# Attention gated by a dequantized FFN: Wo's row factors taken on ScalarE, an earlier schedule for gates and the last queries, and half a projection finished later

## The chip, the core and the metric

The kernel runs on one core of a Trainium2 chip. The metric is the device time of one execution in microseconds. Before the change three runs gave 1065.36, 1066.66 and 1067.37 us, a median of 1066.66 us.

## What is computed

The reference, cut to what matters (S = 1024 tokens, DM = 512, 32 query heads, 8 key and value heads, head size 128, FF = 1792):

```python
xn = _layernorm(x)
q = rmsnorm(split_heads(xn @ Wq.T), q_norm_w)          # 32 heads
k = rmsnorm(split_heads(xn @ Wk.T), k_norm_w)          # 8 heads
v = split_heads(xn @ Wv.T)
bias = where(rel > 0, -1e30, slopes * rel)             # causal, a slope per head
attn = softmax(q @ k.T / sqrt(128) + bias)
s = merge_heads(attn @ v) @ Wo.T
gate = silu(xn @ dequant(gate_w)); up = xn @ dequant(up_w)
g = silu((gate * up) @ dequant(down_w))
return x + s * g
```

## The kernel before

Everything runs in four engines' hand-written order: what a source line issues first stands first on its engine, and nothing is reordered. Floats go through the matrix engine as pairs of f16 (a high and a low part), so each product is three matmuls (`mm3`, L112). ScalarE usually makes the high part and VectorE the low one.

**The FFN** (0 to about 217 us) comes first. Its result, the gate, is stored to DRAM (`gd`), 256 KB for 128 tokens.

**Twelve projections** follow (about 217 to 490 us): for each pair of key heads one of kind `kv` and two of kind `q`, k = 0 to 11. Each has eight tiles of 128 tokens (`tile`, L570): twelve matmuls of 512 columns into one PSUM bank, `o` for odd tiles and `m` for even ones, two buffers each; ScalarE copies the bank to SBUF (`f`) and sums its squares (`jk`), and for `kv` VectorE makes the values' low half (`v`, L595). Every four tiles `queue_half` (L767) queues a finish: `inverse` and `newton` (the roots: a few small operations on VectorE and twelve on GpSimd), then per tile `normalize` (GpSimd, L636), two steps later `halves` (VectorE, a cast L648 and a subtraction L649), then `transposed` (a DMA transpose on SyncE's queue, L657) and `store` (L662). `finish_step` (L477) runs what is due at each step of a clock; it counts one for each tile and one for each attention step.

While projection k runs, `prepare` (L671) makes the weights of k+1 ready, at tile t: `norms` at t = 1 (a small matmul into a spare bank, then VectorE), `scale` at 2, `split_head` i at t = 2 + i (ScalarE `wh` L561, VectorE `wl` L562), `split_values` at 4 and 5, `factors` at 6; at t = 6 also the squares of k+2 (ScalarE). The spare bank is one of tag `m` (`spare`, L486). A projection's first tile needs all of `wh` and `wl`.

**Attention** has 256 steps, 32 to each group g (one key head and four query heads). A group is cut into blocks of eight steps by query block qb of 256 tokens, in the order 2, 3, 0, 1 (group 0: 3, 2, 1, 0; group 7: 2, 3, 1, 0); a step is one head and one tile of 128 queries against (2 qb + 1 or 2 qb + 2) x 128 keys, so qb3 steps are the longest. `step(n)` (L1018) issues: scores of n on the matrix engine into a bank pair `s`; for step n-1 the bias and row minimum (VectorE, `pf` L878) and the exponential (ScalarE, L879); for n-3 the scaled high half `p` (ScalarE, L898); for n-4 the low half (VectorE, L907) and the DMA transpose into `pT` (SyncE's queue, L915 or L910); for the unit of n-9 the product with V (`av`); the output projection `op` and its sum `y` (VectorE, L980). Steps 0 to 7 run among the tiles of projections 10 and 11. In qb0 blocks GpSimd clears `p` first (L894).

**Wo's rows**: 32 tiles of 128x512, four a group. `load_wo` (L832) issues the DMA on SyncE's queue at the end of a step, `scale_wo` (L836) multiplies by a factor for each partition two steps later on GpSimd, `split_wo` (L839) two steps after that (ScalarE `woh` L843, GpSimd `wol` L844). In groups 1 to 7 these stand in the qb3 block and the one after it.

**Projection 11** (the queries of group 7) is not stored: `LAST_ROOTS` and `LAST_PAIRS` (L56) give the attention steps of its roots and of its eight tiles' `halves` (`normalize` two steps before), and `LAST_QUERIES` those of the transposes from SBUF straight into `qT` (L817). Its `f` tiles stay in SBUF until then; the tag has three buffers.

**Gates**: `GATE_LOADS` are the steps at which a query block's gate and x (two DMAs of 512 KB, L962 and L963) are loaded into an `f` buffer, `GATE_SUMS` those at which GpSimd forms y times gate plus x (L969, L970; two tiles, four operations).

Of the kernel before, what the change touches and what calls it, by code (L numbers as in the profile page):

```python
# [10 lines left out]
F32 = mybir.dt.float32  # L11
F32R = mybir.dt.float32r
F16 = mybir.dt.float16
BF16 = mybir.dt.bfloat16
I32 = mybir.dt.int32
AF = mybir.ActivationFunctionType
ALU = mybir.AluOpType
# [4 lines left out]
P = 128  # L22
S = 1024
DM = 512
# [3 lines left out]
HD = 128  # L28
FF = 1792
NI = FF // P  # L30
# [5 lines left out]
NQT = QB // P  # L36
# [16 lines left out]
VALUES_STEP = 24  # L53


LAST_ROOTS = {1: 24, 0: 36}  # L56
LAST_PAIRS = {4: 46, 5: 78, 6: 110, 7: 142, 2: 174, 3: 221, 0: 224, 1: 229}
LAST_QUERIES = {4: 217, 5: 219, 6: 225, 7: 227, 2: 233, 3: 235, 0: 241, 1: 243}

WO_SPLIT = 6  # L60
WO_SCALE = 8
WO_LOAD = 10

GATE_LOADS = [211, 219, 235, 251]
GATE_SUMS = [227, 235, 251, 259]
PF_BUFS = 5
P16_BUFS = 5
OH_BUFS = 8
# [8 lines left out]
def attention_gated_by_ffn_kernel(ctx, tc, x, gu_w, gu_z, gu_s, dn_w, dn_z, dn_s, wq, wkv, wo, qnw, knw, out):  # L77
    nc = tc.nc
    ve, se, ge, te, sp = nc.vector, nc.scalar, nc.gpsimd, nc.tensor, nc.sync
# [5 lines left out]
    def ps2(name):  # L85
        return psum[0].tile([P, 2, 512], F32, tag="s", name=name)

    def ps1(tag, name):
        return psum[0].tile([P, 512], F32, tag=tag, name=name)
# [22 lines left out]
    def mm3(ps, lhs, rhs, first, last):  # L112
        (lh, ll), (rh, rl) = lhs, rhs
        te.matmul(ps, lhsT=lh, rhs=rh, start=first, stop=False)  # L114
        te.matmul(ps, lhsT=lh, rhs=rl, start=False, stop=False)  # L115
        te.matmul(ps, lhsT=ll, rhs=rh, start=False, stop=last)  # L116
# [12 lines left out]
    rvs = const.tile([P, HKV], F32, name="rvs")  # L129
# [30 lines left out]
    def pair(name):  # L160
        return fpsum.tile([P, 2, 512], F32, tag="pair", name=name)
# [267 lines left out]
    def dn_dequant(it, engine=ge):  # L429
        wi, wf, zi, si = dn_raw[it]  # L430
        ve.tensor_tensor(wf, wi, zi, ALU.subtract)
        engine.tensor_tensor(wf, wf, si, ALU.mult)
# [9 lines left out]
    def dn_split_h(it, tb):  # L442
        hh = gp.tile([P, 512], F32R, tag="hh", name=f"hh{it}_{tb}", bufs=3)
        hl = gp.tile([P, 512], F32R, tag="hl", name=f"hl{it}_{tb}", bufs=3)
        split_r(h[:, it, tb * 512 : tb * 512 + 512], hh, hl)
        dn_h_hl[it, tb] = (hh, hl)
# [36 lines left out]
    def defer(steps, f):  # L483
        finishing.setdefault(clock[0] + steps, []).append(f)

    def spare(k, name):  # L486
        return ps1("m", name) if k else pair(name)[:, 0, :]

    class Projection:
        def __init__(self, k, kind, i):  # L490
# [147 lines left out]
        def halves(self, t):  # L638
            f = self.f[t // HT][:, t % HT]
            n = self.n  # L640
            if self.kind == "q":
                a16 = fq.tile([P, 2, n, HD], F16, tag="a16", name=f"q16_{self.i}_{t}", bufs=5)
                hi, lo = a16[:, 0], a16[:, 1]
            else:
                a16 = fq.tile([P, 2, 2, HD], F16, tag="a16", name=f"k16_{self.i}_{t}", bufs=5)
                hi, lo = a16[:, :, 0, :], a16[:, :, 1, :]
                ve.tensor_tensor(f, f, wn.unsqueeze(1).to_broadcast([P, 2, HD]), ALU.mult)
            ve.tensor_copy(hi, f)  # L648
            ve.tensor_tensor(lo, f, hi, ALU.subtract)  # L649
            if self.k == len(projections) - 1:  # L650
                last_pairs[t] = a16
            else:
                defer(1, lambda: self.transposed(t, a16))
# [12 lines left out]
    projections = []  # L666
# [4 lines left out]
    def prepare(k, t):  # L671

        if k < len(projections):
            p = projections[k]
            if t == -1:
                p.squares()
            elif t == 1:
                p.norms()
            elif t == 2:
                p.scale()  # L680
            elif t == 6:
                p.factors()
            if 2 <= t < 2 + p.n:
                p.split_head(t - 2)
            elif p.kind == "kv" and 4 <= t < 6:
                p.split_values(t - 4)

    def down_begin():
        dn_split_w(0)
# [4 lines left out]
    for it in range(3, NI):  # L694
        if it < 3 + 2 * KT:
            projections[(it - 3) // KT].load((it - 3) % KT)
        last = it == NI - 1
        gu_unit(
            it,
            None,  # L700
            it + 1 if not last else None,
            meanwhile={NI - 2: lambda: dn_dequant(0, ve), NI - 1: down_begin}.get(it, lambda: None),
            total=not last,
        )
        if it == NI - 5:
            prepare(0, -1)
        if it == NI - 4:
            prepare(0, 1)
        if it == NI - 3:
            dn_load(0)  # L710
            dn_load(1)
        if last:
            dn_load(2)
            dn_split_h(0, 1)
# [3 lines left out]
    for it in range(NI):  # L718
        for tb in range(2):
            if it == 0:  # L720
                two = [pair(f"dn_ps{tb}_{i}") for i in range(2)]
                acc[tb] = [two[i // 2][:, i % 2, :] for i in range(4)]
            if tb == 0:
                if it + 2 < NI:
                    dn_dequant(it + 2)
                if it + 3 < NI:
                    dn_load(it + 3)
                if it + 1 < NI:
                    dn_split_w(it + 1)
            if it + 1 < NI:  # L730
                dn_split_h(it + 1, tb)
            wh, wl = dn_w_hl[it]
            hh, hl = dn_h_hl.pop((it, tb))
            for i in range(4):
                c = slice(i * P, i * P + P)
                mm3(acc[tb][i], (hh[:, c], hl[:, c]), (wh, wl), it == 0, it == NI - 1)
            if tb:
                if 0 <= it - 3 < HKV:
                    wo_squares_load(it - 3)
                if 0 <= it - 5 < HKV:  # L740
                    wo_squares(it - 5)
                if it in (1, 2):
                    gu_total((NI - 1, None), it - 1)
                elif it == 3:
                    gu_finish(0)
                elif it == 4:
                    gu_finish(1)
                elif it == 5:
                    norm_weights()
                elif NI - 6 <= it < NI - 1:  # L750
                    prepare(0, 8 - NI + it)
                if it == NI - 2:
                    prepare(1, -1)
            if it == NI - 1:
                for i in range(4):
                    go = h[:, i, tb * 512 : tb * 512 + 512]
                    se.activation(go, acc[tb][i], AF.Silu)
                    sp.dma_start(gd[tb * 4 + i], go)
# [5 lines left out]
    fq = ctx.enter_context(tc.tile_pool(name="finish", bufs=2, side="right"))  # L764
    ap1 = ctx.enter_context(tc.tile_pool(name="attn1", bufs=2, side="right"))

    def queue_half(p, half):  # L767

        last = p is projections[-1]

        def due(steps, i, f):
            if last and i is None:
                c = TILES + LAST_ROOTS[half]
            elif last:
                c = TILES + LAST_PAIRS[half * HT + i] - 4
            else:
                c = clock[0] + (i or 0)
            finishing.setdefault(c + steps, []).append(f)

        due(0, None, lambda: p.inverse(half))  # L780
        if p.by_root:
            due(1, None, lambda: p.newton(half, True))
        else:
            for i in range(3):
                due((i + 1) // 2, None, lambda i=i: p.newton(half, i == 0))
        for i in range(HT):
            t = half * HT + i
            due(4, i, lambda t=t: p.halves(t))
            due(2, i, lambda t=t: p.normalize(t))
# [5 lines left out]
    trel, pT, oT, wor = {}, {}, {}, {}  # L795
# [38 lines left out]
        sp.dma_start(wor[g, i], wo[(g * NH + i) * HD : (g * NH + i + 1) * HD, :])  # L834

    def scale_wo(g, i):  # L836
        ge.tensor_scalar(wor[g, i], wor[g, i], rvs[:, g : g + 1], None, ALU.mult)  # L837

    def split_wo(g, i):  # L839
        woh[g, i] = late[0].tile([P, DM], F16, tag="woh", name=f"woh{g}_{i}", bufs=5)  # L840
# [116 lines left out]
    gates = {}  # L957

    def gate_load(qb):
        gx = fq.tile([P, 2, NQT, DM], F32, tag="f", name=f"gx{qb}", bufs=3)  # L960
        t0 = qb * NQT
        sp.dma_start(gx[:, 0], gd[t0 : t0 + NQT].rearrange("t p c -> p t c"))  # L962
        sp.dma_start(gx[:, 1], x[t0 * P : (t0 + NQT) * P, :].rearrange("(t p) c -> p t c", p=P))  # L963
        gates[qb] = gx
# [27 lines left out]
    for k, (g, qbs) in enumerate(blocks[:-1]):  # L992
# [5 lines left out]
        n, taken, done = max(free, due), 0, 0  # L998
        op_first.setdefault(g, n)
        for qb in qbs:  # L1000
            for i in range(NQT):
                for part in range(NH):
# [5 lines left out]
                    if taken == 2 or n < due + done:  # L1008
                        n, taken = n + 1, 0
        free = n + (taken > 0)  # L1010
    late, y_ = [], []
    TILES = NT * len(projections)
# [5 lines left out]
    def step(n):  # L1018
# [39 lines left out]
        if done is not None and units[done][:2] == final:  # L1058
# [5 lines left out]
            if hh == NH - 1:  # L1064
                for due in acc_at.get(nn + AV_LAG + 1, ()):
                    accumulate(*due, other=True)
                for i in range(NQT):
                    accumulate(g, qb, i)
        if n in GATE_LOADS:
            gate_load(LAST_ORDER[GATE_LOADS.index(n)][0])  # L1070
        for i in range(NQT):
            if n - i in GATE_SUMS:
                gate_partial(LAST_ORDER[GATE_SUMS.index(n - i)][0], i)
        for lead, act in ((WO_SPLIT, split_wo), (WO_SCALE, scale_wo), (WO_LOAD, load_wo)):
# [78 lines left out]
```

## Time and profile before

| what | value |
|---|---|
| median of three runs | 1066.66 us |
| the profiled execution: its time, its span | 1066.42 us, 1064.6 us |
| busy: PE, VectorE, ScalarE, GpSimd | 1002.7, 886.1, 802.7, 413.9 us |
| p low half, VectorE L907, x256 | 227.8 us |
| bias and minimum, VectorE L878, x256 | 207.2 us |
| exponential, ScalarE L879, x256 | 197.6 us |
| Wo factor, GpSimd L837, x32 | 54.5 us, mean 1702 ns |
| mean granted PE clock | 0.993 |

The profile is of one execution; its own time is 0.24 us under the median. PE is the matrix engine, DVE is VectorE, ACT is ScalarE, POOL is GpSimd, SPq is SyncE's queue, from which all DMAs here are issued. [...]

### The profile page before, as it was taken

What the parts mean: (1) busy time and instruction counts of PE and PEld (TensorE: products, weight loads), DVE (VectorE), ACT (ScalarE), POOL (GpSimd) and SP (SyncE); (2) the same over time, 40 slices, a digit from 0 to 9 for tenths busy, and PEclk for the clock granted to TensorE, in tenths of its full rate; (3) what the DMA queues carried; (4) which work ended last, traced back from release to release, by engine and by line L of the source; (5) the groups of instructions that cost most, each with busy time, mean ns of one, the idle gap of its engine ahead of it and who ended that gap; (6) DMA issues with size and microseconds to landing.
All of it is one profiled execution on the core that took longest, in us unless ns stands there. A gap on an engine that the chain in (4) does not pass through costs nothing.

```text
span 1064.6 us, 18405 instructions
## 1 busy us (share of the span) xinstructions
PE 1002.7 (94%) x5913; PEld 584.6 (55%) x5913; DVE 886.1 (83%) x1745; ACT 802.7 (75%) x2160; POOL 413.9 (39%) x407
## 2 busy tenths in 40 slices
PE   7899899999989999898799999999999999999986
PEld 4344377844444444344566666566666666665563
DVE  7888996638778687788799899898998998979986
ACT  5777644778877787587778788797987888868862
POOL 2588653124545546361343215123141141250732
PEclk9999999999999999999999999999999999999998
DMA  6123259447988989989999999899999998999995
GB/s 202 49 100 119 70 170 302 166 139 162 219 228 188 242 203 235 279 179 207 226 193 214 195 200 222 167 227 197 189 207 193 197 223 182 221 224 194 231 189 129
DMA packets 455039, 204.39 MB, mean 192 GB/s; under 512 B 401506, under 2 KB 411038, under 8 KB 454942
## 3 DMA queue, kind: packets, MB, share of 16 engines
q1 hardware_dynamic: 454942, 203.21, 85.4%
q8 instruction: 46, 0.75, 0.3%
q14 instruction: 51, 0.42, 0.1%
HBM read 77.32 MB, written 27.27 MB: 98 GB/s over the span
## 4 chain that ended last, share of the span: by engine, by line
PE 48%; DVE 17%; ACT 13%; issue 10%; DMA 8%; SPq 2%; POOL 2%; DVEq 0%; ACTq 0%; POOLq 0%
PE gu_ps L267 6%; DMA pT<-p 4%; PE s L114 4%; DVE pf L878 3%; PE s L116 3%; PE s L115 3%; PE op L114 3%; PE op L115 3%; PE av L114 3%; PE op L116 3%; PE av L116 3%; PE av L115 3%; ACT p L898 2%; ACT pf L879 2%; PE ps_q L114 2%
## 5 line engine op out<-in xcount | busy, mean ns | idle before, releaser
L907 DVE SCALAR_TENSOR_TENSOR p<-pf,row,p 128x1024 f16<-128x1024 f32 (+7 forms) x256 | 227.8, 890 | 23.5 <-ACT p L898 20.3
L879 ACT ACTIVATE pf<-pf,row 128x1024 f32<-128x1024 f32 (+7 forms) x256 | 197.6, 772 | 57.2 <-DVE row L878 52.7
L878 DVE CUSTOM_DVE_ANT_0 pf<-s,trel,cs 128x1024 f32<-128x1024 f32 (+7 forms) x256 | 207.2, 809 | 13.7 <-PE s L116 13.4
L898 ACT ACTIVATE p<-pf,row 128x1024 f16<-128x1024 f32 (+7 forms) x256 | 196.5, 768 | 8.4 <-DMA pT<-p 3.5
L114 PE MATMUL av<-pT,vT 128*128 128x256 f16 (+1 forms) x640 | 167.8, 262 | 15.5 <-DMA pT<-p 15.5
L115 PE MATMUL av<-pT,vT 128*128 128x256 f16 (+1 forms) x640 | 167.8, 262 | 0.0
L116 PE MATMUL av<-pT,vT 128*128 128x256 f16 (+1 forms) x640 | 167.6, 262 | 0.0
L114 PE MATMUL s<-kT,qT 128*128 128x512 f16 (+3 forms) x384 | 125.0, 325 | 12.4 <-DVE row L878 12.1
L115 PE MATMUL s<-kT,qT 128*128 128x512 f16 (+3 forms) x384 | 125.0, 326 | 0.0
L116 PE MATMUL s<-kT,qT 128*128 128x512 f16 (+3 forms) x384 | 123.4, 326 | 0.0
L837 POOL TENSOR_SCALAR wor<-wor,rvs 128x512 f32<-128x512 f32 x32 | 54.5, 1702 | 162.8 <-DMA wor<-in_wo 141.5
L114 PE MATMUL ps_q<-wh_q,xth 128*128 128x512 f16 x256 | 97.6, 381 | 2.6 <-DVE am_q L526 2.5
L116 PE MATMUL ps_q<-wh_q,xtl 128*128 128x512 f16 x256 | 97.5, 381 | 0.0
L115 PE MATMUL ps_q<-wl_q,xth 128*128 128x512 f16 x256 | 97.5, 381 | 0.0
L114 PE MATMUL op<-woh,oh 128*128 128x512 f16 x248 | 94.5, 381 | 0.0
L115 PE MATMUL op<-wol,oh 128*128 128x512 f16 x248 | 94.3, 380 | 0.0
L116 PE MATMUL op<-woh,ol 128*128 128x512 f16 x248 | 94.2, 380 | 0.0
L114 PEld LDWEIGHTS <-vT 128*128 128x128 f16 x640 | 62.6, 98 | 56.6 <-DMA pT<-p 9.4
L115 PEld LDWEIGHTS <-vT 128*128 128x128 f16 x640 | 62.6, 98 | 41.3 <-issue 3.5
L941 ACT ACTIVATE oh<-av 128x256 f16<-128x256 f32 x128 | 47.7, 373 | 48.5 <-PE av L116 47.8
L636 POOL TENSOR_TENSOR f_q<-f_q,inv_q 128x512 f32<-128x512 f32 x64 | 77.4, 1237 | 1.1
L844 POOL TENSOR_TENSOR wol<-wor,woh 128x512 f16<-128x512 f32 x32 | 49.4, 1543 | 71.3 <-ACT woh L843 71.3
(194 smaller groups left out, 2255.6 us busy)
## 6 DMA issues: line engine op xcount, KB each, us to landing
qd<-tr_q SPq DMA_DIRECT2D x56, 256.0 KB, 3.4
qT<-qd SPq DMA_DIRECT2D x28, 512.0 KB, 4.5
wq<-in_wq SPq DMA_DIRECT2D x32, 256.0 KB, 3.9
wo_sq<-in_wo SPq DMA_DIRECT2D x8, 1024.0 KB, 9.1
wor<-in_wo SPq DMA_DIRECT2D x32, 256.0 KB, 3.7
gui<-in_gu_w SPq DMA_DIRECT2D x13, 512.0 KB, 3.5
wkv<-in_wkv SPq DMA_DIRECT2D x16, 256.0 KB, 3.8
vd<-v SPq DMA_DIRECT2D x8, 512.0 KB, 4.0
```

Source lines behind the costliest of these rows:

```text
L114: te.matmul(ps, lhsT=lh, rhs=rh, start=first, stop=False)
L115: te.matmul(ps, lhsT=lh, rhs=rl, start=False, stop=False)
L116: te.matmul(ps, lhsT=ll, rhs=rh, start=False, stop=last)
L267: te.matmul(banks[j][:, k, :], lhsT=w[:, j, ws], rhs=x[:, j, k * 512 : k * 512 + 512], start=x is xth, stop=x is xtl)
L636: ge.tensor_tensor(f, f, ib, ALU.mult)
L837: ge.tensor_scalar(wor[g, i], wor[g, i], rvs[:, g : g + 1], None, ALU.mult)
L844: ge.tensor_tensor(wol[g, i], raw, woh[g, i], ALU.subtract)
L878: ve.tensor_tensor_reduce(p, ps, trel[g][:, S - w :], cs[:, hh : hh + 1], 3e38, ALU.add, ALU.min, least[:, c])
L879: se.activation(p, p, AF.Exp, bias=least[:, c], scale=-1.0, accum_out=total[:, c])
L898: se.activation(p16[u, qt][:, :, 0, :], pf[u, qt], AF.Copy, scale=scale[:, qt : qt + 1])
L907: ve.scalar_tensor_tensor(lo, p, scale, hi, ALU.mult, ALU.subtract)
L941: se.activation(oh, av_ps[u], AF.Copy, scale=1.0 / P_SCALE)
```

## The change

Six edits in one:

- `scale_wo` is issued on ScalarE instead of GpSimd, at the same steps.
- `norms`, `scale`, `split_head`, `split_values` and `factors` come one tile later. The spare bank of `norms` is of the scores' tag `s`; for projection 11, in whose preparation scores already run, of tag `o`.
- The second half (tiles 4 to 7) of projection 10, the queries of group 6, is finished in attention's group 1: roots from step 28, `halves` at 36, 44, 52 and 60, each with its transpose one step and its store three steps later. Before, this followed the tiles at once.
- Projection 11's roots move from steps 24 and 36 to 66 and 70, its pairs from 46, 78, 110, 142, 174, 221, 224, 229 to 76, 88, ..., 160, twelve apart. Three of the pairs use buffers of tag `tr`, since all eight now lie in SBUF at once.
- Gate loads move from 211, 219, 235, 251 to 194, 203, 211, 219 (query blocks 2, 3, 1, 0), sums from 227, 235, 251, 259 to 221, 229, 244, 237.
- The gate tile of query block 0 has a buffer of its own.

```diff
-LAST_ROOTS = {1: 24, 0: 36}
-LAST_PAIRS = {4: 46, 5: 78, 6: 110, 7: 142, 2: 174, 3: 221, 0: 224, 1: 229}
+LAST_ROOTS = {1: 66, 0: 70}
+LAST_PAIRS = {4: 76, 5: 88, 6: 100, 7: 112, 2: 124, 3: 136, 0: 148, 1: 160}
+LATE_ROOTS = 28
+LATE_PAIRS = [36, 44, 52, 60]
...
-GATE_LOADS = [211, 219, 235, 251]
-GATE_SUMS = [227, 235, 251, 259]
+GATE_LOADS = [194, 203, 211, 219]
+GATE_SUMS = [221, 229, 244, 237]
...
     def spare(k, name):
-        return ps1("m", name) if k else pair(name)[:, 0, :]
+        if k == 0:
+            return pair(name)[:, 0, :]
+        return ps2(name)[:, 0, :] if k < len(projections) - 1 else ps1("o", name)
...
-                a16 = fq.tile([P, 2, n, HD], F16, tag="a16", name=f"q16_{self.i}_{t}", bufs=5)
+                tag = "tr" if self.k == len(projections) - 1 and t in (0, 1, 3) else "a16"
+                a16 = fq.tile([P, 2, n, HD], F16, tag=tag, name=f"q16_{self.i}_{t}", bufs=5)
...
-            elif t == 1:
+            elif t == 2:
                 p.norms()
-            elif t == 2:
+            elif t == 3:
                 p.scale()
-            elif t == 6:
+            elif t == 7:
                 p.factors()
-            if 2 <= t < 2 + p.n:
-                p.split_head(t - 2)
-            elif p.kind == "kv" and 4 <= t < 6:
-                p.split_values(t - 4)
+            if 3 <= t < 3 + p.n:
+                p.split_head(t - 3)
+            elif p.kind == "kv" and 5 <= t < 7:
+                p.split_values(t - 5)
...
+        late = p is projections[-2] and half == 1
         def due(steps, i, f):
-            if last and i is None:
+            if late:
+                c = TILES + (LATE_ROOTS if i is None else LATE_PAIRS[i] - 4)
+            elif last and i is None:
...
     def scale_wo(g, i):
-        ge.tensor_scalar(wor[g, i], wor[g, i], rvs[:, g : g + 1], None, ALU.mult)
+        se.activation(wor[g, i], wor[g, i], AF.Copy, scale=rvs[:, g : g + 1])
...
     def gate_load(qb):
-        gx = fq.tile([P, 2, NQT, DM], F32, tag="f", name=f"gx{qb}", bufs=3)
+        pool, tag, bufs = (fq, "f", 3) if qb else (late[0], "gx", 1)
+        gx = pool.tile([P, 2, NQT, DM], F32, tag=tag, name=f"gx{qb}", bufs=bufs)
```

More of the change, by code (lines that the diff above doesn't have):

```diff
@@ L707, in attention_gated_by_ffn_kernel @@
         if it == NI - 4:
-            prepare(0, 1)
+            prepare(0, 2)
         if it == NI - 3:
@@ L750, in attention_gated_by_ffn_kernel @@
                 elif NI - 6 <= it < NI - 1:
-                    prepare(0, 8 - NI + it)
+                    prepare(0, 9 - NI + it)
                 if it == NI - 2:
```

## The prediction

> **What bounds the kernel now.** I read the page's busy row first, then what the matrix engine (PE) waited for, stretch by stretch, then the granted clock around its longest waits, and last the chain of waits in order of time.
>
> The page's busy row:
>
> ```profile
> PE 1002.7 (94%) x5913; PEld 584.6 (55%) x5913; DVE 886.1 (83%) x1745; ACT 802.7 (75%) x2160; POOL 413.9 (39%) x407
> ```
>
> PE is the bound, so a gain has to come out of PE's waits. The waits of PE in the projections (213 to 490 us), the start of attention (485 to 532), its middle (532 to 1000) and its end (1000 to 1065):
>
> ```profile
> PE n_ps L518 <- DVE v L595: 5.6, 3, 2.7
> PE ps_q L114 <- DVE am_q L526: 2.5, 2, 1.2
> ...
> PE av L114 <- DMA pT<-p: 5.9, 5, 2.6
> PE s L114 <- DVE row L878: 4.7, 5, 1.8
> ...
> PE s L114 <- DVE row L878: 6.7, 13, 0.8
> PE av L114 <- DMA pT<-p: 3.3, 4, 1.4
> ...
> PE av L114 <- DMA pT<-p: 6.2, 5, 2.7
> PE s L114 <- DVE row L878: 0.7, 1, 0.7
> ```
>
> The columns are total us, times, longest. The first two rows are 8.1 us for the norms' small matmul and its bank. The start of attention holds 10.6 us in 47; the middle loses only 10.0 us in 468; the end 6.9. That is about 36 us in all, the ceiling of any gain here, plus what the clock adds. Windows just behind the two longest waits (PE, PEld, DVE, ACT, POOL busy, then clock, DMA share, GB/s):
>
> ```profile
> 440.00:444.20 4.20, 4.12 (x14) 1.56 (x14) 4.03 (x12) 2.24 (x15) 0.00 (x0) 0.66 1.05 247
> ...
> 1044.20:1047.40 3.20, 3.19 (x13) 1.63 (x14) 3.10 (x6) 0.56 (x2) 1.48 (x2) 0.57 0.79 161
> ```
>
> After idling 2.7 us PE had only 0.66 and 0.57 of its clock: another 1.4 us each. The chain in order of time (start, us, what), start of attention and end:
>
> ```profile
> 510.10 1.04 SPq L915
> 511.25 1.36 SPq L915
> 512.67 4.50 DMA wor<-in_wo
> 517.26 2.11 POOL wor L837
> 525.75 5.73 DMA pT<-p
> ...
> 1030.74 1.28 POOL y L969
> 1033.69 1.68 POOL y L969
> 1037.14 7.02 DMA pT<-p
> ```
>
> At 510 to 531 the path runs through SyncE's queue and Wo's rows; at the end through the gate sums on GpSimd and a transpose that lands after 7.0 us where its neighbours need 3 to 4.5.
>
> **Norms a tile later, in another bank.** Removed: the waits at 305.03 (1.46 us, and 1.24 at 309.05 for the same bank), the like pair at 371.7, 0.3 at 327.6, and 2.71 at 440.07 with 1.4 of slow clock. Added: no instruction, but the weights' last quarter comes a tile later. In projection 3 `wl_q` ends at 300.08 and the tile that needs it starts at 300.82: 0.74 us of slack, and as little at 366.8 and 432.7. By the built order its `wh` (0.70) now follows tile 5's evacuation, 300.22 to 300.9, and its `wl` follows that tile's v, cast, subtraction and reciprocal, which ended at 301.98; with 0.7 for itself it ends at 302.7, so the first tile waits 1.9 us. Net: 2.7 - 1.9 = 0.8, twice, plus 0.3. At 440 it is 2.71 + 1.4 - 1.9 = 2.2, but VectorE is busy almost without pause from 439.6 to 476.1 and scores wait for it, so I keep 0.8. Query and kv projections after a query one have 2.8 to 4.2 us of slack against 2.6 us of shift: nothing. Sum: gain 3; bounds 0 (VectorE binds all) and 6 (the split stands earlier than I place it).
>
> [...]
>
> **Half of projection 10 moved out of the start.** Each of its four pairs issues `normalize` on GpSimd (mean 1.24 us), cast and subtraction on VectorE (means 0.59 and 0.83; 0.42 and 0.69 with GpSimd silent), a transpose (1.28 us of SyncE's queue) and a store (0.54 to 1.03). Before, VectorE ended a low half at 476.10, idled 2.72 us for GpSimd, then did four pairs until 487.7, with the next `pf` at 484.40; ScalarE idled 4.35 us for that and then worked from 485.72 to 496.78 without a gap. Its scores had ended by 474, so these 4.35 us go. On SyncE's queue, busy without a gap from 493 to 531 and up to 6.5 us behind VectorE's low halves, 5.2 us of transposes and 2.8 of stores go, which should cover half of the 5.9 us of `pT` waits: 2.7. Sum: gain 7; bounds 2 and 10.6, all of the stretch.
>
> In group 1 the four pairs and the roots come back: one falls into the qb0 block, where VectorE is busy 12.6 of 17.5 us, and costs nothing; one pair leaves (step 46); two remain, 1.1 us each if nothing hides them. The roots' twelve GpSimd operations lie in its idle time. The stores pass 60 steps of transposes on SyncE's queue, and group 6 loads them some 120 steps later. Cost 1; bounds 0 and 4 (pairs slowed by GpSimd, two more DMAs in the qb3 block).
>
> **Wo's factor on ScalarE.** GpSimd loses 32 x 1.70 = 54.5 us. A low half (128x1024) beside GpSimd's work took 1.82 us at 720.74, alone 1.26 at 713.88; over all 29 that overlap a factor this is 6.0 us, most of it under a busy PE. ScalarE gains 32 instructions; nearest row, `p` 128x512 by the same function and factor, 707 ns (copies 609, with bias 806): 2.8 us a group, three of four in the qb3 block. In 700 to 725 ScalarE is busy 21.3 of 25 us, so 2.1 more just fits.
>
> The new wait: ScalarE now stops for the row's DMA, 3.2/3.7/5.6 us from issue to landing. Behind it are queued `oh`, the next exponential and `p`, and behind these VectorE's low half, the transpose and `av`. From the timeline (end of the instruction now ahead against landing) in groups 1 to 6 the row is in first by up to 3.6 us, in two of 24 late by at most 0.65. Group 0 is late by 0.9 to 4.9, but there SyncE's queue is itself behind, with two or three transposes ready to issue while ScalarE stands, and ScalarE's waits for GpSimd (3.9 us) end: I count 2 us, inside the 7 above.
>
> **Pairs, roots, gates.** Five pairs stood in qb3 blocks. Groups 3 and 5 lose theirs: their block took 23.0 us, group 6's without one 21.8. Half is kept, because PE was busy all along; with the silent GpSimd I take 2 us for groups 2 to 5, bounds -3 (ScalarE binds) and 6.
>
> At the end, the loads at 235 and 251 go: 1 MB each that stood before transposes 3.7 us long, landing after 7.6 and 7.0 us. `pT` waits at 1005 to 1025 are 3.6 us, of which 2.5 should go (queries and Wo's rows still use the queue). The gate sums leave the qb0 block: low halves of 256 took 1062 ns there against 464 alone, and the 2.7 us wait at 1044 with its clock (1.4) should mostly go: 3. Pairs at 221 to 229 leave too: group 6's qb1 block took 16.3 us against 13.5 elsewhere, but gate sums and two loads come in: 1. Sum 6.5; bounds 2 and 10.
>
> **Sum.** 3 + 7 - 1 + 2 + 6.5 = 17.5. From the profiled execution's 1066.42 this gives 1048.9, and its median is 0.24 higher: 1049.0.
>
> **Rivals.** *The bound only changes hands at the start* (0.17): SyncE's queue has 31 us of transposes from step 4 to 15 whatever VectorE does, and Wo's rows queue behind them, so the 7 becomes 1 and the new first-tile wait eats the 3: about 1058. For it: the unbroken queue. Against it: 8 us of that queue's work leaves.
>
> *PE never waits* (0.10): starts, ends and qb0 blocks all close, 31 of 36 us: 1035. Against it: the middle's waits come from VectorE, whose work stays.
>
> *ScalarE stands for Wo's rows* (0.09): if transposes delay the loads, each factor costs 0.7 + w, four times in each of six groups, against the 3.3 us that ScalarE has to spare in a block. It decides at 6 x (4 x (0.7 + w) - 3.3) = 15.5, what the other edits give: w = 0.8 us. With the 2 us seen late in group 7 it would be 45, less 15.5: 1096; at 1.2 us, 1076. Slower. Against it: the margins above.
>
> *The edits cancel* (0.03): group 1 and the splits cost what the start gives: 1066.
>
> **Numbers.** My forecast has 0.61, within 1042 to 1056. Faster by over 0.2%, about what a measurement of this kernel can tell from no change, is 0.61 + 0.17 + 0.10 = 0.88; the same 0.03; slower 0.09. The range leaves out the slower case and half of the fastest: 1036 to 1064.
>
> **What would show it.** Right: no wait at the small matmul but about 2 us at the first tile of projections 4, 7 and 10; the exponential of step 16 at about 513 us instead of 520; ScalarE waiting for `wor` in group 0 only; pieces of GpSimd gone from the end of the chain, the clock there at 1.00. Wrong: ScalarE idle for `wor` over 0.8 us per row, a qb3 block over 23 us, or the start's `pT` waits still near 6 us.

## The result, and the profile after

The changed kernel took 1075.16 us (median of four runs, 1072.60 to 1075.83) beside 1067.01 us for the kernel before (four runs, 1065.36 to 1069.40). The ratio is 1.0065, 95% interval 1.0042 to 1.0087: slower by some 7 us, where 17 us of gain were forecast. The profiled execution took 1075.83 us, with a span of 1073.9 us against 1064.6.

The page's busy row of the changed kernel:

```profile
PE 1006.7 (94%) x5913; PEld 586.2 (55%) x5913; DVE 881.7 (82%) x1745; ACT 818.8 (76%) x2192; POOL 351.5 (33%) x375
```

ScalarE has its 32 instructions more, GpSimd 62 us less, VectorE 4 us less. Two engines have less to do and the kernel is slower: the row can't say why. PE's waits in the changed kernel, stretch by stretch (projections, start of attention, middle, end; columns total us, times, longest):

```profile
PE ps_q L117 <- ACT wh_q L566: 6.5, 3, 3.3
PE ps_q L118 <- DVE wl_q L567: 3.8, 3, 1.3
...
PE s L117 <- DVE row L888: 5.1, 5, 1.7
...
PE s L117 <- DVE row L888: 16.0, 28, 1.9
PE av L117 <- DMA pT<-p: 9.3, 9, 2.3
...
PE av L117 <- DMA pT<-p: 0.9, 1, 0.9
PE op_last L119 <- DVE ol L956: 0.6, 1, 0.6
```

The waits at the norms' small matmul are gone (8.1 us), but 10.3 us stand at the first tiles. The start lost its waits for `pT` (5.9 us), the end 5.3 of its 6.2. The middle went from 10.0 us to 25.3. In all, PE's waits from 213 us on grow from 38.0 to 43.5 us and its busy time by 4.0 (at half its clock a matmul of 512 columns is busy 0.63 us, as at 305.02 in the changed kernel, where at full clock it is busy 0.38, as at 307.84): 9.5 us, beside 9.2 of span. The chain of the changed kernel (start, us, what), at the start of attention, in group 6 and at the end:

```profile
508.98 1.11 SPq L925
510.15 3.16 DMA wor<-in_wo
...
911.26 8.13 DMA pT<-p
...
931.96 5.89 DMA wor<-in_wo
...
952.49 5.27 DMA pT<-p
...
959.30 5.28 DMA pT<-p
...
1033.19 5.11 DMA pT<-p
...
1056.39 0.69 DVE gx L995
```

GpSimd has left the end of the chain, as forecast, and the granted clock near the end is 1.00 from 1044 to 1056 us and 0.97 from there to 1073, where before it was 0.88 from 1036 to 1050 and again from there to 1064. Group 6 has four long DMAs on the chain; before, it had one (5.49 us).

To see where the 9.2 us of span come from I took the start of each stage's first score or projection matmul in both traces, so that the stages are measured on PE, the engine that bounds. Differences after less before, in us:

| stage | forecast | trace |
|---|---|---|
| up to the first tile of projection 11 | -3 | +4.1 |
| from there to step 32 (group 1) | -7 | -6.0 |
| group 1 | +1 | +5.7 |
| groups 2 to 5 | -2 | +6.9 |
| group 6 | -1 | +5.5 |
| group 7 and the tail | -5.5 | -6.9 |
| sum | -17.5 | +9.2 |

The two gains came as forecast. Everything else has the wrong sign or size.

Groups 1 to 6 lose 18.1 us, and 13.0 of them lie in one block of four, qb0. The length of the blocks by the same measure:

| block | before | changed kernel, difference |
|---|---|---|
| qb3, groups 1 to 6 | 21.77, then 21.79 each | +1.37, +0.24, 0.00, 0.00, 0.00, +1.49 |
| qb1, groups 1 to 5 | 12.68 each | +0.21, 0.00, +0.21, 0.00, 0.00 |
| qb0, groups 1 to 6 | 19.07, 19.34, 18.13, 18.35, 18.94, 18.22 | +3.56, +2.02, +0.46, +2.15, +0.47, +4.35 |

The qb3 block, in which my prediction looked for the cost, takes 21.79 us in groups 3 to 5 in every kernel of this study, and PE is busy for nearly all of it. What VectorE or ScalarE can't finish there is paid in the qb0 block behind it. In groups 1 and 6 the qb3 block itself is longer as well.

### The profile page after: what moved, and what is told of

Read it like the earlier page. It is cut to its first block, busy times and chain, and to the rows that moved or that the text cites. A ratio compares the mean times of both kernels' runs of the same rounds, so it can differ in the third digit from the quotient of the medians.

```text
span 1073.9 us, 18383 instructions
## 1 busy us (share of the span) xinstructions
PE 1006.7 (94%) x5913; PEld 586.2 (55%) x5913; DVE 881.7 (82%) x1745; ACT 818.8 (76%) x2192; POOL 351.5 (33%) x375
## 4 chain that ended last, share of the span: by engine, by line
PE 42%; DVE 19%; ACT 18%; issue 10%; DMA 9%; SPq 1%; POOL 1%; DVEq 0%; ACTq 0%; POOLq 0%
PE gu_ps L270 6%; DMA pT<-p 5%; DVE pf L888 5%; ACT p L908 4%; ACT pf L889 4%; DVE p L917 3%; PE ps_q L118 3%; PE ps_q L119 3%; PE ps_q L117 2%; PE av L117 2%; PE s L117 2%; PE s L119 2%; PE s L118 2%; PE av L119 2%; PE av L118 2%
## 5 line engine op out<-in xcount | busy, mean ns | idle before, releaser
L917 DVE SCALAR_TENSOR_TENSOR p<-pf,row,p 128x1024 f16<-128x1024 f32 (+7 forms) x256 | 224.8, 878 | 29.8 <-ACT p L908 27.2
L117 PE MATMUL av<-pT,vT 128*128 128x256 f16 (+1 forms) x640 | 167.6, 262 | 10.3 <-DMA pT<-p 10.1
L956 DVE SCALAR_TENSOR_TENSOR ol<-av,oh 128x256 f16<-128x256 f32 x128 | 53.4, 418 | 27.7 <-ACT oh L951 26.6
L641 POOL TENSOR_TENSOR f_q<-f_q,inv_q 128x512 f32<-128x512 f32 x64 | 74.9, 1193 | 1.0
```

Source lines behind the costliest of these rows:

```text
L641: ge.tensor_tensor(f, f, ib, ALU.mult)
L917: ve.scalar_tensor_tensor(lo, p, scale, hi, ALU.mult, ALU.subtract)
L956: ve.scalar_tensor_tensor(ol, av_ps.pop(u), 1.0 / P_SCALE, oh, ALU.mult, ALU.subtract)
```

## The experiments

Theory A at the outset: each loss belongs to the edit that works in its stage (the delayed weights in the projections, the late half in group 1, the factors in the middle, the gates' loads in group 6). The rival was that the factors on ScalarE are behind all of the middle's loss. Each timed kernel has its own runs of the kernel before beside it; every ratio is to those, with its 95% interval.

**One edit undone at a time.** Four kernels, each the changed one less an edit.

```diff
prep_sooner:    norms, scale, split_head, split_values, factors: t as in the kernel before; new spare bank kept
factor_gpsimd:  - se.activation(wor[g, i], wor[g, i], AF.Copy, scale=rvs[:, g : g + 1])
                + ge.tensor_scalar(wor[g, i], wor[g, i], rvs[:, g : g + 1], None, ALU.mult)
half_at_once:   - late = p is projections[-2] and half == 1
                + late = False
gates_before:   + GATE_LOADS = [211, 219, 235, 251];  GATE_SUMS = [227, 235, 251, 259]
```

> The changed kernel, except that the preparation of the next projection's weights stands one tile sooner again, where it stood before; the new spare bank stays. Theory A (the tile of delay is what the projections lose): the waits of 11.6 us for the split weights at the first tiles of projections 4, 7 and 10 go, those for the norms' bank don't come back, and the time falls 8 to 12 us below the changed kernel's 1075. Rival (VectorE is full in the projections, and the wait only moves): less than 4 us, with PE waiting as long for VectorE at other lines.

> The changed kernel, except that Wo's factors are multiplied on GpSimd again. Theory A (ScalarE pays for the factors and for the waits at their rows in groups 1 to 6): the steps 32 to 223, which grew by some 11 us, lose most of that, and the time falls by 8 to 11 us. Rival (the late half and the moved pairs are what groups 1 and 4 to 6 pay for, the factor is hidden): within 3 us of the changed kernel's 1075, or slower, because the low halves on VectorE are stretched by GpSimd again.

> The changed kernel, except that the second half of projection 10 is finished at once again, in the start of attention. Theory A (group 1 pays for the late half): steps 32 to 63 lose 5 to 6 us, the start grows by about 6, and the time stays within 2 us of the changed kernel's 1075. Rival (group 1 pays for Wo's factors on ScalarE): steps 32 to 63 lose at most 1.5 us, the start grows by about 6, and the time rises by 4 to 6 us.

> The changed kernel, except that the gates' loads and sums stand at their steps of before (211, 219, 235, 251 and 227, 235, 251, 259). Theory A (the loads at 194 and 203 hold up SyncE's queue, and so Wo's rows, in group 6's qb3 block): steps 192 to 223 lose 4 to 5 us, the end grows by as much, and the time stays within 2 us of the changed kernel's 1075. Rival (group 6 pays for Wo's factors or for its own VectorE work): steps 192 to 223 lose at most 1.5 us, the end grows by 4 to 6, and the time rises by 3 to 6 us.

| kernel | median us | ratio to before |
|---|---|---|
| prep_sooner | 1073.94 | 1.0054 (1.0035 to 1.0073) |
| factor_gpsimd | 1077.56 | 1.0079 (1.0058 to 1.0100) |
| half_at_once | 1078.41 | 1.0096 (1.0074 to 1.0118) |
| gates_before | 1076.55 | 1.0073 (1.0052 to 1.0093) |

No single edit is the culprit: none of the four comes near the kernel before. With half_at_once, group 1 is 5.3 us shorter, as theory A said, and steps 8 to 31 are 6.1 us longer; the time is some 3 us longer. So the late half is worth about 3 us (the two intervals overlap, but every run of half_at_once is slower than every run of the changed kernel), and in group 1 the pairs are most of what is paid. With the factors back on GpSimd (factor_gpsimd), 4.5 of the 5.7 us stay. With gates_before, group 6 is 4.0 us shorter and group 7 with the tail 5.3 us longer: the early loads gain and lose about the same. With factor_gpsimd, groups 1 to 5 are 3.9 us shorter in the trace and group 6 is 2.2 longer. In its runs nothing is gained: the time is what the rival said, though in the trace the factor isn't hidden. prep_sooner gave 1 of the 8 to 12 us that theory A expected. Its trace shows why: the first tile of projection 10 starts 6.9 us earlier than in the changed kernel, but by step 8 only 1.0 us of that is left. At the preparation of projection 11, whose spare bank is the other one (`o`), PE stands twice, 2.5 us for ScalarE's sums of squares and 2.7 for VectorE's `v`.

**One edit alone.** Three kernels, the one before plus one edit; shift_alone is the delayed preparation with the new bank, pairs_gates_alone the steps below.

```diff
factor_alone:       scale_wo on ScalarE
pairs_gates_alone:  LAST_ROOTS, LAST_PAIRS, GATE_LOADS, GATE_SUMS and their buffers as in the changed kernel
shift_alone:        norms at t = 2 ... factors at t = 7; spare bank of tag s (o for projection 11)
```

> The kernel before with one edit: Wo's factors on ScalarE. Theory A (each group pays 1 to 2 us for the four factors in its qb0 block, as the traces of the changed kernel with and without them show in groups 2 to 4): 5 to 9 us slower than before. Rival (what the factors take on ScalarE, the silent GpSimd gives back on VectorE): within 2 us of before, or faster by up to 3.

> The kernel before, with only the last projection's pairs and roots and the gates' loads and sums of the change. Theory (twelve steps apart puts the roots into group 2's qb2 block, and pairs into the qb0 blocks of groups 3 and 4, and the loads stand before the transposes of group 6's qb3 block): groups 2 to 5 lose 2 to 4 us, group 6 loses 5 to 8, the last two blocks gain 6 to 8, in sum 0 to 4 us slower than before. Rival (the end's gain is what this edit brings, the losses belong to the other edits): groups 2 to 6 lose less than 2 us in sum and the time is 5 to 7 us below before.

> The kernel before with only the first edit (the preparation a tile later, the new spare bank); three pairs use the buffers of tag tr and one gate tile its own, as in the changed kernel. Theory (first-tile waits of 3 to 4.6 us at projections 4, 7 and 10 take the place of waits of 2.7): attention's step 8 starts 3 to 5 us later than before and the time is 2 to 5 us above before. Rival (VectorE gives the lost time back in attention's start, where before it was the bound anyway): step 32 within 1.5 us of before, and the time within 2 us.

| kernel | median us | ratio to before |
|---|---|---|
| factor_alone | 1069.73 | 1.0031 (1.0015 to 1.0047) |
| pairs_gates_alone | 1070.38 | 1.0024 (1.0014 to 1.0034) |
| shift_alone | 1073.88 | 1.0059 (1.0041 to 1.0077) |

All three make the kernel slower by themselves. The shift is the largest: 0.59% is 6.3 us where I had forecast 3 of gain. The prices alone aren't shares, though: undoing the shift in the changed kernel (prep_sooner) gave back 0.11%, not 0.59. With the half's gain (0.0096 less 0.0065 is 0.31%) the four give 0.59 + 0.31 + 0.24 - 0.31 = 0.83%, and 0.65% was measured, which the intervals allow. pairs_gates_alone went as its theory said: groups 2 to 5 lost 3.5 us, group 6 6.9, and group 7 with the tail gained 6.5. factor_alone ended between its two theories. Of shift_alone's loss only 2.9 us stand at step 8 of its trace; the rest came later, 1.8 in the qb2 block of group 0 and 1.0 to 1.8 in three later blocks. So part of the loss isn't where I looked for it. The mean granted clock of that execution is 0.988, beside 0.993 before; how much of the loss in these blocks is the clock's is left open.

**Where the pairs stand.** pairs_qb1 moves all twelve pairs into qb1 blocks, two to a block; prep_mixed leaves the preparation where it stood before for all projections but 11, whose preparation alone comes a tile later; best1 has both, and all gate loads in qb1 blocks.

```diff
pairs_qb1:  + LATE_PAIRS = [58, 61, 90, 93];  LAST_ROOTS = {1: 118, 0: 182}
            + LAST_PAIRS = {4: 122, 5: 125, 6: 154, 7: 157, 2: 186, 3: 189, 0: 218, 1: 221}
            + GATE_LOADS = [194, 203, 223, 211]
prep_mixed: + if t >= 0 and k < len(projections) - 1: t += 1      (in prepare)
best1:      both, with GATE_LOADS = [187, 191, 223, 219]
```

> The changed kernel, but the late half's pairs stand at 58, 61, 90 and 93 and the last projection's at 122, 125, 154, 157, 186, 189, 218 and 221 (roots at 118 and 182), so that all of them lie in qb1 blocks; two gate loads follow their buffers (211 for query block 0, 223 for query block 1). Theory (a pair in a block where VectorE is full is paid in the next qb0 block, while a qb1 block has 2 us of VectorE to spare): the qb0 blocks of groups 1, 2 and 4 lose 1.5 to 3 us each, no qb1 block gains more than 0.7, and the time falls by 4 to 8 us from the changed kernel's 1075. Rival (the factors on ScalarE and the transposes are what the qb0 blocks pay for): the qb0 blocks keep all but 0.5 us each, and the time stays within 2 us.

> The changed kernel, but the preparation of projections 0 to 10 stands one tile sooner again, in the new bank; only projection 11's comes a tile later. Theory (the tile of delay costs projections 4, 7 and 10 their first tiles, while the sooner preparation of projection 11 cost 3.8 us because its spare bank of tag o was still in use): the first tile of projection 10 starts 5 to 7 us sooner than in the changed kernel, the first tile of attention's step 8 as well, and the time falls by 4 to 6 us from 1075. Rival (VectorE carries the lost time on into attention's start): the gain at projection 10 is gone by step 16 and the time falls by less than 2 us.

> Both of these together, with the gate loads at 187, 191, 223 and 219, all in qb1 blocks. If the costs lie in separate stages they add: 1075 less 6 for the pairs, less 5 for the preparation, less 3 to 4 for the loads out of group 6's qb3 block: about 1061, below the 1067 to 1069 of before. Rival (the loads only move their wait to group 6's qb2 block, and the factors keep their cost): 1066 to 1070.

pairs_qb1: 1076.79 us, 1.0095 (1.0075 to 1.0115), slower than the changed kernel; prep_mixed: 1073.43, 1.0060 (1.0040 to 1.0080), no gain that can be told; best1: 1068.32, 1.0012 (1.0003 to 1.0021), 5.7 us better than the changed kernel by the ratios, and where its rival put it. In pairs_qb1 the qb0 blocks of groups 1 and 4 did lose 3.3 and 2.8 us, but that of group 2 grew by 0.7, and each qb1 block of groups 1 to 5, with two pairs in place of one or none, grew by 1.3 to 1.5 us, every time to 1.49 or 1.50 over before. A qb1 block of group 3 with two pairs (best1) and with one (late_one_a_block, below), by window; columns: PE, PEld, DVE, ACT, POOL busy, then clock, DMA share, GB/s:

```profile
740.97:755.15 14.18, 12.96 (x83) 7.46 (x81) 12.55 (x34) 9.20 (x26) 2.98 (x7) 1.00 0.67 153
```

```profile
737.00:749.88 12.88, 12.88 (x83) 7.45 (x81) 10.87 (x32) 9.12 (x26) 0.00 (x0) 1.00 0.71 170
```

With one pair PE is busy for all of the block's 12.88 us. With two, VectorE has 12.55 us to do and PE stands for 1.22: the first pair costs 0.20 in this block (12.88 against 12.68), the second 1.30. Not all of the 1.30 need be VectorE's two operations: GpSimd works 2.98 us here and not at all in the other block, and in the kernel before a low half of 256 columns took 1.06 us beside GpSimd's gate sums (1034 to 1048 us, mean of four), where in a block of the changed kernel without GpSimd's work it took 0.47 (at 749.19). That share was not tried apart.

So two kernels with one pair to a qb1 block and one to a qb3 block, with best1's preparation and gate loads, differing in who multiplies Wo's rows:

```diff
spread_act:  + LATE_PAIRS = [46, 60, 78, 92];  LAST_ROOTS = {1: 95, 0: 159}
             + LAST_PAIRS = {4: 110, 5: 124, 6: 142, 7: 156, 2: 174, 3: 188, 0: 206, 1: 220}
spread_pool: the same, scale_wo on GpSimd
```

> The changed kernel with projection 11's preparation alone a tile later, gate loads at 187, 191, 223 and 219, the late half's pairs at 46, 60, 78 and 92, and the last pairs at 110, 124, ..., 220 (roots at 95 and 159): one pair to a qb1 block and one to a qb3 block of groups 1 to 6, none in qb0 or qb2. Theory (the first pair in a qb1 block costs 0 to 0.2 us and the second 1.3 to 1.5; the pair in a qb3 block costs under 1 in the qb0 block behind it): six second pairs save 1.3 to 1.5 each and cost up to 0.7 in the qb0 blocks, so 4 to 6 us below the 1068 of the kernel with two pairs in each qb1 block: 1062 to 1064. Rival (a pair costs the same wherever VectorE has less than 2 us to spare): within 2 us of 1068.

> The same with Wo's factors on GpSimd. Theory (the factors on ScalarE cost about 0.3% alone, where the kernel before had only them changed): 2 to 3 us below the same kernel with the factors on ScalarE, 1059 to 1062. Rival (with the pairs out of the full blocks ScalarE has the time, and GpSimd's factors stretch VectorE's low halves instead): the same or up to 3 us more.

1069.06 us, 1.0006 (0.9992 to 1.0020), and 1068.49, 1.0010 (0.9995 to 1.0026). Neither theory's gain came; both times are the rivals'. The second pairs did go (0.20 to 0.51 in the qb1 blocks of groups 1 to 5 of spread_act), and the qb0 blocks of groups 1, 2 and 4 took 2.4, 4.0 and 1.0 us over before. The pairs in the qb3 blocks of groups 1 to 5 stand at the steps at which the kernel before has its own, so they don't explain this. What does is open.

**One pair to a block, and the end.** late_one_a_block starts from the kernel before instead: prepare as in prep_mixed, the late half at one pair in each qb1 block of groups 1 to 4, everything else as before (but for the new spare bank and the buffers that the pairs need). late_and_end adds the last three pairs and the gates in a form that puts one load ahead of group 6's qb3 block.

```diff
late_one_a_block: + LATE_PAIRS = [60, 92, 124, 156]; three buffers for the roots; rest as before
late_and_end:     + LAST_PAIRS = {4: 46, 5: 78, 6: 110, 7: 142, 2: 174, 3: 188, 0: 206, 1: 220}
                  + GATE_LOADS = [211, 219, 223, 191];  GATE_SUMS = [221, 229, 244, 237]
```

> The kernel before with two edits in another form: the preparation in the new bank but only projection 11's a tile later, and the late half of projection 10 with one pair in each of the qb1 blocks of groups 1 to 4 (steps 60, 92, 124, 156; roots at 28); factors, last pairs and gates as before. Theory (the loss in the middle comes from where pairs stand): the start ends 5 to 7 us sooner, each of the four qb1 blocks gains 0.2, the other blocks of groups 2 to 6 stay as before, and the time is 4 to 6 us below before, 1061 to 1063. Rival (the two kernels with pairs elsewhere lost at group 1's and 2's qb0 blocks because the half's transposes and stores pass SyncE's queue there): those blocks gain 2 to 4 us each and the time is within 2 us of before.

> The kernel late_one_a_block with the last three pairs at 188, 206 and 220 instead of 221 to 229, and the gates' loads at 191, 211, 219 and 223, their sums at 221, 229, 237 and 244. Theory: the end gains 5 to 7 us as in all kernels with early gates, and group 6 loses under 2 because only one load stands in front of its qb3 block: 3 to 5 us below late_one_a_block. Rival (the loads cost in group 6 what they save at the end, wherever they stand, because the DMA engines are full there): within 2 us of late_one_a_block, with group 6 longer by 4 to 7 us.

late_one_a_block: 1069.39 us, 1.0011 (0.9998 to 1.0025). Its trace agreed with its theory in part (steps 8 to 31 5.4 us shorter, each of the four qb1 blocks 0.20 longer), its runs did not: 22 executions lie between 1063.97 and 1073.81, the profiled one at 1065.47. In the trace the qb0 blocks of groups 1 to 6 lost 0.7 to 1.8 us each, 6.3 in sum. late_and_end: 1064.30 us, 0.9975 (0.9962 to 0.9987): faster than both kernels. Here group 6 loses 0.6 us in place of 5.5, and group 7 with the tail gains 4.7. Group 1 (qb2, qb3, qb0, qb1) in the changed kernel, and in late_one_a_block, with the columns as above:

```profile
558.78:581.92 23.14, 21.95 (x138) 13.07 (x138) 21.24 (x38) 19.84 (x36) 1.37 (x2) 1.00 1.13 215
581.92:604.55 22.63, 17.47 (x142) 12.82 (x141) 17.80 (x42) 16.76 (x44) 7.29 (x9) 1.00 1.07 207
```

```profile
553.33:575.10 21.77, 21.62 (x140) 13.01 (x138) 21.44 (x38) 19.43 (x35) 8.40 (x6) 1.00 1.06 211
575.10:594.85 19.75, 17.44 (x143) 12.79 (x141) 16.59 (x39) 14.94 (x41) 7.31 (x9) 1.00 1.12 209
```

The first line of each is the qb3 block, the second the qb0 block behind it. PE has 17.4 us to do there in both. In the changed kernel VectorE has 1.2 us more and ScalarE 1.8, and the block takes 2.9 us longer.

**The two terms still open.** wl_later is late_and_end with only the low half of the weights' split (`wl`, VectorE) a tile later, for projections 0 to 10; late_and_end_act is late_and_end with the factors on ScalarE; wl_later_act is both.

```diff
wl_later:          + split_low(t - 4) apart from split_head(t - 3), which keeps wh   (k < 11)
late_and_end_act:  + se.activation(wor[g, i], wor[g, i], AF.Copy, scale=rvs[:, g : g + 1])
```

> The kernel late_and_end, but of the weights' split only the low half (VectorE) comes a tile later for projections 0 to 10; the high half (ScalarE) stays. Theory (two adjacent waits make the clock fall, one alone doesn't): the first tiles of projections 4 and 7 wait for wl alone, 1 to 2.5 us each, the clock in the 4 us behind it stays above 0.95, and the time rises by 2 to 5 us over late_and_end's 1064.3. Rival (any wait of that length at this place slows the clock): the clock behind it falls to 0.5 to 0.7 for 3 us, and the time rises by 5 to 9 us.

> The kernel late_and_end with Wo's factors on ScalarE. Theory (their cost alone was 0.31%, most of it in attention's start): 2 to 4 us slower than late_and_end, with ScalarE waiting 5 to 9 us for the rows. Rival (with the other edits in place the factors cost nothing, as undoing them in the changed kernel suggests): within 1.5 us of it.

> The kernel wl_later with Wo's factors on ScalarE. Theory (the two edits work at different places, the projections and the middle): the gains add, about 1060, 0.65% below before. Rival (both shorten the same waits in attention's start): within 1 us of wl_later, 1061 to 1063.

| kernel | median us | ratio to before |
|---|---|---|
| wl_later | 1062.13 | 0.9953 (0.9941 to 0.9965) |
| late_and_end_act | 1062.13 | 0.9959 (0.9947 to 0.9972) |
| wl_later_act | 1064.69 | 0.9977 (0.9961 to 0.9994) |

wl_later has the lowest ratio of this study, 0.5% under before and 1.1% under the changed kernel (0.9953/1.0065); late_and_end_act lies within its interval. On the clock its theory held at projections 4 and 7: waits of 1.0 and 2.7 us for `wl` alone, and behind them a clock of 1.00 (302.70 to 306.70 and 368.30 to 374.50 us). At projection 10 PE waited 2.9 us for `wl`, and the clock fell to 0.71 and 0.50. The kernel before, too, has one wait of the same 2.7 us, at 440, and behind it the clock is 0.50 over 1.93 us: so adjacent waits aren't what it takes. What parts these cases is left open. Windows of the wait at projection 7 and the 2.2 us behind it, then the 4.3 us behind the wait at projection 10:

```profile
365.40:368.30 2.90, 0.19 (x1) 0.00 (x0) 2.18 (x5) 2.80 (x12) 0.58 (x1) 1.00 1.10 295
368.30:370.50 2.20, 2.19 (x11) 1.00 (x11) 0.28 (x1) 2.17 (x12) 1.87 (x7) 1.00 1.10 256
...
434.66:437.00 2.34, 2.34 (x8) 0.94 (x8) 0.00 (x0) 1.65 (x5) 2.01 (x7) 0.71 1.14 347
437.00:439.00 2.00, 2.00 (x6) 0.76 (x5) 0.00 (x0) 1.94 (x9) 0.93 (x2) 0.50 1.15 297
```

On the time it was wrong: 2 us less instead of 2 to 5 more. The waits of late_and_end at the norms' matmuls, 1.2 us at 325, 1.7 at 392 and 3.6 at 443, are not in wl_later's trace, and those for `wl` in their place sum to 6.7: the delay moved waits, and cost nothing. Why it is faster in sum was not tried. late_and_end_act was no slower than late_and_end, so in this setting the factors on ScalarE cost nothing, though alone they cost 0.31%. The two don't add: wl_later_act fits neither expectation. Its ratio is 0.24% above wl_later's, with intervals that overlap. Its profiled execution, one of its slower runs (1069.31), lost 3.7 us in the qb0 block of group 2, where wl_later lost 0.5. The mean granted clock of that execution was 0.988, wl_later's 0.992; how much of the 3.7 is the clock's is left open.

## Why the prediction was wrong, point by point

**What bounds the kernel** was right: PE is the bound, and the 9.2 us show up as its waits and its clock. Against the forecast the stages miss by 8.9 us in groups 2 to 5, 7.1 in the projections, 6.5 in group 6 and 4.7 in group 1.

**The norms' step failed:** "With 0.7 for itself it ends at 302.7, so the first tile waits 1.9 us", from which I took a gain of 3, bounds 0 to 6. In the changed kernel's trace the stage loses 4.1 us; by itself the edit costs 0.59%, 6.3 us, the most of the three edits tried alone. Two terms were mis-sized. First, the wait: PE waits twice, for `wh` and one matmul later for `wl`, 1.4 + 1.3 us at projection 4, 1.8 + 1.3 at projection 7 and 3.3 + 1.3 at projection 10. I had counted only `wl`, at 302.7, and put `wh` at 300.9; but ScalarE's copy of the tile ahead of it began 1.1 us later than before, so `wh` ended at 302.1 and `wl` at 303.7. Second, the clock. Behind the two waits at projection 4 of the changed kernel, and around the two norms' waits of the kernel before:

```profile
302.16:303.79 1.63, 0.38 (x2) 0.10 (x2) 1.54 (x4) 1.57 (x5) 0.59 (x1) 1.00 0.32 118
303.79:306.00 2.21, 2.21 (x6) 0.83 (x6) 0.00 (x0) 2.15 (x11) 1.88 (x7) 0.51 0.88 210
306.00:308.00 2.00, 2.00 (x8) 0.76 (x7) 1.67 (x4) 1.33 (x8) 1.06 (x2) 0.69 0.08 30
```

```profile
305.00:307.00 2.00, 1.97 (x11) 0.91 (x11) 1.96 (x4) 0.58 (x4) 0.78 (x1) 1.00 0.01 4
309.00:312.00 3.00, 2.96 (x14) 1.36 (x14) 2.11 (x9) 2.86 (x16) 0.64 (x4) 1.00 0.94 238
```

Before, waits of 1.46 and 1.24 us stood 4 us apart and the clock stayed at 1.00. In the changed kernel as much idle time stands around a single matmul, and the clock falls to 0.51 and 0.69: 2.21 x 0.49 + 2.0 x 0.31 = 1.7 us lost, and about as much at projections 7 (a clock of 0.60 and 0.80 from 371.50 to 374.50 and on to 377.00) and 10 (0.89, 0.50 and 0.95 from 439.09 to 440.72, 443.50 and 446.00). Nor is that this trace's luck alone: in shift_alone, whose weights come as late, the clock behind the first tile of projection 4 was 0.58 over 2.20 us and 0.60 over the next 2.00. So 10.3 us of waits and some 5.1 of clock took the place of 8.1 us of waits and 1.4 of clock: 15.4 - 9.5 = 5.9. Another 1.1 us of small waits of the kernel before went too, which leaves 4.8, beside the 4.1 of the stage table. I had priced the clock in what went away and not in what came.

**The start's step was right**: 7 forecast, bounds 2 to 10.6, 6.0 found. half_at_once shows that it is the half's doing: steps 8 to 31 are 6.1 us longer without it. Its sign of success, the exponential of step 16 at 513, was wrong (519.14 against 520.20), because the stage began 4 us later and the chain still runs over SyncE's queue and Wo's row at 509 to 513.

**Group 1's step failed**: "one falls into the qb0 block, where VectorE is busy 12.6 of 17.5 us, and costs nothing", in sum 1, bounds 0 to 4. It cost 5.7. The room in the qb0 block isn't free: VectorE comes to it late from the qb3 block, where it is busy 21.4 of 21.8 us already in the kernel before, and PE waits at its scores. A sign of being wrong came here as well: the qb3 blocks of groups 1 and 6 took 23.1 and 23.3 us, over the 23 I had named. With the half at once group 1 gains 5.3 of the 5.7 back; with one pair, in the qb1 block, it costs 0.9.

**Wo's factors and the middle**: "I take 2 us for groups 2 to 5, bounds -3 (ScalarE binds) and 6" as a gain; they lost 6.9. In the traces 2.7 of that goes with the factors back on GpSimd, and pairs_gates_alone has 3.5 by itself: +1.3, -1.0, +0.7 and +1.4 in the qb0 blocks of groups 2 to 5, the rest elsewhere. Which pair costs which can't be read from that: group 3's qb0 block has a pair and is shorter, group 5's has none and is longer. My working looked at the qb3 blocks by VectorE's instructions (23.0 and 21.8 us). By PE they last 21.79 in groups 3 to 5 with a pair (before) and without one (the changed kernel), so a pair removed there couldn't show there. The instruction's price was right (718 ns against 707), and the rows' DMA was not the cost: ScalarE's waits for it by stretch (485 to 540, 540 to 620, 620 to 900, 900 to 1000 us) were

```profile
ACT wor L847 <- DMA wor<-in_wo: 1.3, 1, 1.3
...
ACT wor L847 <- DMA wor<-in_wo: 2.4, 1, 2.4
...
ACT wor L847 <- DMA wor<-in_wo: 0.5, 1, 0.5
...
ACT wor L847 <- DMA wor<-in_wo: 4.0, 3, 1.7
```

6.9 us over the 24 rows of groups 1 to 6 is 0.29 us a row, under the 0.8 at which that rival decides. So the slower rival that I wrote out is not what happened; what happened, several full blocks each losing a little, I had only as "the edits cancel" with 0.03.

**The end's step was right, but its price was left out.** Group 7 and the tail gained 6.9 (5.5 forecast), and the clock there is 1.00 up to 1056 us. I counted the loads at 235 and 251 as gone; they are moved, to 194 and 203, ahead of the block in which the DMA share is 1.06 already before (909.35 to 931.14 us). Behind the load at 194 a transpose takes 8.13 us on the chain, behind that at 203 Wo's row 5.89, and group 6 loses 5.5 us. In late_and_end, without a load at 194, no DMA on the chain takes over 5.52 us from 890 to 966, and in the kernel before none over 5.49. gates_before gives 4.0 of it back; with 191, 211, 219 and 223 (and other last pairs) group 6 loses 0.6.

What stays open: why the factors on ScalarE cost 0.31% alone and nothing in three other settings (the changed kernel, spread_act, late_and_end_act); which edits make the losses of groups 2 to 5, of which the traces place only part; and why executions of one kernel differ by 2 to 12 us, which makes a single trace a poor witness for 2 us.

## What to carry to other kernels

Price what an edit moves at its new place as carefully as at its old one: a wait that is moved can bring a slow clock of its own (1.7 us behind the two waits at projection 4 here), and a load or a vector operation that leaves one block costs what the block that receives it has no room for. Measure stages by the instructions of the engine that is the bound; a block that is full on another engine looks unharmed and sends the bill to the next. Room is where PE never waits and the feeding engine idles, here 2 us of VectorE in a qb1 block: one pair there cost 0.2 us, a second 1.3.

## What the runs showed of the hardware

In these traces the length of PE's idle time doesn't by itself tell whether the clock falls. PE's waits, and the granted clock just behind them:

| kernel and place | PE's waits, us | granted clock behind |
|---|---|---|
| wl_later, projection 7 | 2.7 | 1.00 over 2.20 us |
| kernel before, at 305 and 309 | 1.46 and 1.24, 4 us apart | 1.00 over 2.00 and 3.00 us |
| kernel before, at 440 | 2.7 | 0.50 over 1.93 us |
| wl_later, projection 10 | 2.9 | 0.71 over 2.34 us, then 0.50 over 2.00 |
| changed kernel, at 302 | 1.4 and 1.3, with one matmul between | 0.51 over 2.21 us, then 0.69 over 2.00 |

The wait at 440, whose windows stand nowhere above (columns as there):

```profile
436.00:440.07 4.07, 1.36 (x9) 0.59 (x6) 0.48 (x2) 3.94 (x18) 2.18 (x4) 0.92 1.16 306
440.07:442.00 1.93, 1.93 (x7) 0.77 (x7) 1.86 (x5) 0.55 (x4) 0.00 (x0) 0.50 1.09 251
```

Two waits of the same 2.7 us had a clock of 1.00 and of 0.50 behind them. What decides between the two is left open, so whether a wait of this length costs the clock as well was known here only from the trace.

A pair that VectorE does in 1.1 us (0.42 and 0.69, at 755.58 and 756.03 in the changed kernel) cost PE 0.20 us as the first and 1.30 as the second in a 12.7 us block, to within 0.01 us in most groups. And in group 6 the load of the next keys took 9.3 us to land beside the gate loads of the changed kernel and 9.5 in pairs_gates_alone, against 5.2 before and 5.0 in late_and_end.
